# Batch 1's low-rank product of a gated block-sparse layer: sixteen folds replaced by four pairs of seven block products

## The chip, the cores and the metric

The kernel runs on one core of one Trainium2 chip. Its engines are named as in the profile: PE (matrix engine), DVE (vector), ACT (scalar), POOL (GpSimd) and SP (SyncE, which only issues DMAs here). The metric is device time in microseconds (us) of the whole program, as the median of several runs.

## The reference, cut to what matters

`xn` is the layer-normed input `x`, of 2 batches of 1024 rows and 1024 columns. A masked linear layer gives `s`, a linear layer with eight low-rank experts gives the gate `g`, and the output is `x + s * silu(g)`:

```python
xn = _layernorm(x)
s  = einsum('bsk,nk->bsn', xn, weight * blockmask) + bias
q  = einsum('bi,ki->bk', xn.mean(axis=1), Wq)
coeffs = softmax(einsum('bk,ek->be', q, lora_keys) / sqrt(128))     # 8 experts
h     = einsum('bsi,eir->bser', xn, lora_down)                      # rank 64 each
delta = einsum('be,bser,ero->bso', coeffs, h, lora_up)
out   = x + s * silu(einsum('bsi,oi->bso', xn, W_org) + delta)
```

Since the coefficients depend on the batch only, the kernel folds the experts into the weight. With D the 1024 x 512 matrix of all `lora_down`, U the 512 x 1024 matrix of all `lora_up` and C the diagonal of the coefficients (64 equal ones for each expert), batch b is multiplied by the effective weight `W_org^T + D C_b U`, of 1024 x 1024. The term `D C_1 U`, batch 1's low-rank product, is what the change is about.

## The kernel before, in words

All matrix products are made to fp32 accuracy in three passes. An operand is split into a rounded part "hi" (a copy by ACT) and a remainder "lo" (a subtraction by DVE), and a product is hi*hi + hi*lo + lo*hi: three matmuls with a 128x128 stationary and a 128x512 moving operand. "k tiles" are the eight blocks of 128 rows of the weight, "h" its two halves of 512 columns.

The program first prepares batch 0 and multiplies it as plain tiles (`gemm`: 8 k tiles x 3 matmuls for a 128x512 result). Phase y00 and phase y01 are the gate's two halves for batch 0; S tiles 0 to 7 (`s_tile`) are the last half of `s` for batch 0. Batch 1 comes last, as eight units of weight rows, each done by a `quad`: seven block products in place of eight (Strassen's scheme in Winograd's form), with operand blocks `xw[0]` to `xw[3]` (batch 1's input, each of seven block combinations) and `ow` (the weight's). The combinations of the input were stored in DRAM (`xv`) before; `fill(j, m)` loads one, and splits it into `xw[j]`.

Batch 1's effective weight is built between phase y01 and the quads, and goes to DRAM (`yu`), from where the quads' units of kind "y" load it. That is done in 16 *folds*, one for each h and k tile, which stand between the S tiles 0 to 4 in groups of 4, 4, 3, 3 and 2. A fold loads a D tile (`ds`) and a W_org tile (`wo`), splits D into `dhi` and `dlo` (L410, L411), multiplies it with the four scaled U tiles (`y_mul`: 4 chunks x 3 matmuls, L419 to L421), adds the W_org tile on DVE (`y_sum`, L426) and leaves the result to be stored by an ACT-issued DMA (`store_late`, L515) at the next fold. D is loaded and split twice, once for each h. U is scaled by the coefficients while it is split (`scale_up`, L397 and L398): the first half after batch 1's softmax (`coeffs(1)`, of which `steps` are the parts), the second after fold 7.

Between the folds stand fills of `xw[0]` and then `xw[1]`, through three slots of `misc`, and, as `early`, the masking and the block differences of the quads' unit 0. S tiles 5, 6 and 7 come behind the last fold, with unit 0's splits and two fills.

Order: inside the scheduled region PE, DVE, ACT and POOL execute in the order in which the program is written; SP's DMAs are placed by a planner, which may pull a load ahead of its place in the text. An evacuation of a PSUM tile is put into `pending` and written out at the next `flush`. A final evacuation (`final_evac`) is DVE's sum and product, a POOL-issued DMA that adds x into the tile (L507), and an output store, which is issued by ACT at the start of the next S tile but one (`store_out`, L522). On any engine an instruction that waits holds up all that is behind it, DMA issues included.

Buffers that matter: `raw` (seven slots of 128x512), `misc` (three), `stash` (eight, batch 0's gate tiles until their final evacuation), the pool `cu` (five pairs, U's operands), the pool `stage` (D, W_org and weight tiles); PSUM pools `ps_s` and `ps_w` of two banks each and `ps_acc` of four for the S tiles.

Of the kernel before, what the change touches and what calls it, by code (L numbers as in the profile page):

```python
# [9 lines left out]
F32 = mybir.dt.float32  # L10
F32R = mybir.dt.float32r
# [6 lines left out]
P = 128  # L18
# [14 lines left out]
def kernel(  # L33
# [15 lines left out]
):  # L49

# [602 lines left out]
    with tc.manual_schedule(engines={mybir.EngineType.PE, mybir.EngineType.DVE, mybir.EngineType.Activation, mybir.EngineType.Pool}):  # L653
# [350 lines left out]
        def jobs_c(i):  # L1004
# [6 lines left out]
            if i < 6:  # L1011
                yield J(s_mul, s1, 1, i)
            if i == 6:
                yield steps[3]
                yield J(scale_up, 1, 0, up_homes)
# [12 lines left out]
        up_homes = [misc[:, 0, :]]  # L1028
# [4 lines left out]
        folds = [(h, kt) for h in range(2) for kt in range(NKT)]  # L1033

        def fold(n):
            h, kt = folds[n]
            if n + 1 < len(folds):
                y_prep(1, *folds[n + 1])
            store_late()
            y_mul(1, h, kt)  # L1040
            flush()
            y_sum(1, h, kt)
            ps, ws = staged.pop((1, h, kt))
            late_stores.append((
                yu[:, :, 2 * h + kt // 4, kt % 4, :].rearrange("u p n -> p u n"),
                ws.rearrange("p (u n) -> p u n", n=P),
            ))
            if n == NKT - 1:
                homes = [misc[:, (len(spare) + k) % 3, :] for k in range(3)]
                spare.extend(homes)  # L1050
                scale_up(1, 1, homes)

        xw = {}
        XV = (0, 2, 3, 4, 5, 1, 6)

        def fill(j, m, pool=None, at=None):

            if j not in xw:
                home, tag = ((wpool, "w"), (xpool, "xg"), (xpool, "xg"), (wpool, "w"))[j]
                xw[j] = home.tile([P, 7, 2, NH], F32R, name="xw", tag=tag)  # L1060
            if at is not None:
                st = at
            elif pool is None:
                st = misc[:, len(spare) % 3, :]
# [67 lines left out]
        y_prep(1, *folds[0])  # L1132
        done = 0
        filled = [0, 0]

        def fills(j, n):
            for _ in range(n):
                fill(j, ORDER_X[filled[j]])
                filled[j] += 1

        for i, n in enumerate((4, 4, 3, 3, 2)):
            s_tile(i)
            for k in range(n):
                fold(done)
                done += 1
                if i < 3 and k in ((1, 2, 3), (0, 1), (1, 2))[i]:
                    fills(0, 1)
                if i > 2 and (i == 4 or k):
                    fills(1, 1)
                if (i, k) in ((2, 0), (3, 0), (3, 1), (3, 2), (4, 0), (4, 1)):  # L1150
                    early.pop(0)()
            if i == 0:
# [222 lines left out]
```

## Time and profile before

| what | value |
|---|---|
| median of 3 runs | 445.38 us (444.71 to 446.79) |
| the profiled execution | 444.3 us, span in the profile 442.6 us |
| granted PE clock | 1.00 throughout |
| PE busy | 435.9 us, 2053 matmuls |
| DVE, ACT, POOL busy | 288.0, 174.5, 64.9 us |
| DMA | 90.58 MB, mean 205 GB/s |
| S tile 0 to the first quad | 198.25 to 286.3 us of the span |
| folds and S tiles in it | 16 x 12 and 8 x 24 matmuls |

The profile shows one execution, with times from the start of its span. "Busy" counts the time in which an engine has an instruction in work; matmuls overlap, so PE's pace is read from starts of matmuls and not from the duration of one. A row of the groups gives line, engine, operation, output<-input and mean duration. The chain of waits leads back from the last instruction, at each step to whatever released it.

### The profile page before, as it was taken

The numbers are of one execution on the slowest core, as the hardware profiler recorded it, in microseconds if no ns is written. First come the engines' busy times: TensorE is split into PE (matmuls) and PEld (weight loads), VectorE is DVE, ScalarE is ACT, GpSimd is POOL, SyncE is SP. The second block draws the span as 40 slices with busy tenths as digits, with TensorE's granted clock in tenths as the row PEclk, the third lists the DMA queues.
The fourth block names the chain that finished last, engine by engine and source line by source line (L and its number), as shares of the span: only waits on it lengthen the run. The fifth ranks groups of instructions, "written<-read, shape, count | busy, mean of one in ns | idle before, by whom it ended". The sixth has DMA issues, their size and how long they took to land.

```text
span 442.6 us, 5778 instructions
## 1 busy us (share of the span) xinstructions
PE 435.9 (98%) x2053; PEld 362.7 (82%) x2053; DVE 288.0 (65%) x482; ACT 174.5 (39%) x286; POOL 64.9 (15%) x87
## 2 busy tenths in 40 slices
PE   8999999999999999999999999999999999999996
PEld 6899888888888888888888878888888888888885
DVE  5889977765628778974557568378556395365625
ACT  3787435355721221252232135067335322441510
POOL 3342210002310423210000000110020030002000
PEclk9999999999999999999999999999999999999999
DMA  8994616686896899896988986874183146218103
GB/s 282 392 342 158 205 46 228 217 268 218 236 302 177 275 271 319 298 384 166 296 230 262 320 263 185 252 246 142 43 192 118 64 119 168 95 31 214 42 1 118
DMA packets 47741, 90.58 MB, mean 205 GB/s; under 512 B 4816, under 2 KB 15328, under 8 KB 47712
## 3 DMA queue, kind: packets, MB, share of 16 engines
q1 hardware_dynamic: 30624, 66.08, 44.4%
q0 software_dynamic: 6624, 16.26, 15.5%
q10 hardware_dynamic: 10464, 7.87, 5.4%
q8 instruction: 16, 0.26, 0.2%
q14 instruction: 13, 0.11, 0.1%
HBM read 70.26 MB, written 19.93 MB: 204 GB/s over the span
## 4 chain that ended last, share of the span: by engine, by line
PE 91%; DMA 4%; DVE 2%; ACT 1%; issue 1%; POOL 0%; SPq 0%; ACTq 0%; DVEq 0%
PE acc_ps L1220 25%; PE acc_ps L455 13%; PE acc_ps L459 13%; PE acc_ps L458 13%; PE py L1220 10%; PE psw L419 6%; PE psw L421 6%; PE psw L420 6%; DMA ds<-in_down_dram 3%; DMA raw<-in_x_dram 1%; PE pt L209 0%; DVE s L256 0%; ACT slot L592 0%; POOL slot L596 0%; DVE st L148 0%
## 5 line engine op out<-in xcount | busy, mean ns | idle before, releaser
L1220 PE MATMUL acc_ps<-xw,ow 128*128 128x512 f32 (+1 forms) x492 | 111.9, 384 | 0.0
L455 PE MATMUL acc_ps<-slot,xgrp 128*128 128x512 f32 (+1 forms) x288 | 106.5, 370 | 0.1
L1220 PEld LDWEIGHTS acc_ps<-xw,ow 128*128 128x128 f32 x492 | 90.8, 188 | 18.4
L459 PE MATMUL acc_ps<-slot,xgrp 128*128 128x512 f32 (+1 forms) x288 | 105.5, 366 | 0.2 <-DVE xgrp L608 0.2
L458 PE MATMUL acc_ps<-slot,xgrp 128*128 128x512 f32 (+1 forms) x288 | 105.4, 366 | 0.1
L459 PEld LDWEIGHTS acc_ps<-slot,xgrp 128*128 128x128 f32 x288 | 54.3, 188 | 9.6 <-DVE xgrp L608 0.6
L455 PEld LDWEIGHTS acc_ps<-slot,xgrp 128*128 128x128 f32 x288 | 54.3, 188 | 9.4 <-ACT slot L592 0.6
L458 PEld LDWEIGHTS acc_ps<-slot,xgrp 128*128 128x128 f32 x288 | 54.3, 188 | 8.9 <-POOL slot L596 0.3
L419 PE MATMUL psw<-cut,dhi 128*128 128x512 f32 x128 | 49.9, 390 | 0.3 <-ACT dhi L410 0.3
L421 PE MATMUL psw<-cut,dlo 128*128 128x512 f32 x128 | 49.9, 390 | 0.0
L420 PE MATMUL psw<-cut,dhi 128*128 128x512 f32 x128 | 49.8, 389 | 0.0
L1220 PE MATMUL py<-xw,ow 128*128 128x512 f32 x192 | 46.3, 389 | 0.0
L1220 PEld LDWEIGHTS py<-xw,ow 128*128 128x128 f32 x192 | 36.0, 188 | 7.5
L1113 DVE TENSOR_TENSOR ow<-raw,ow 128x1024 fp32r<-128x1024 f32 (+1 forms) x32 | 34.5, 1088 | 8.6 <-ACT ow L1112 8.6
L410 ACT CAST dhi<-ds 128x512 fp32r<-128x512 f32 x32 | 19.7, 616 | 45.6 <-DMA ds<-in_down_dram 30.2
L507 POOL DMA_DIRECT2D stash<-in_x_dram x16 | 14.4, 899 | 119.8 <-DVE stash L504 119.8
L426 DVE TENSOR_TENSOR wo<-wo,psw 128x512 f32<-128x512 f32 x32 | 21.9, 686 | 13.9 <-PE psw L421 13.5
L1112 ACT CAST ow<-raw 128x1024 fp32r<-128x1024 f32 (+1 forms) x32 | 29.4, 939 | 1.6 <-DVE wo L426 1.6
L419 PEld LDWEIGHTS psw<-cut,dhi 128*128 128x128 f32 x128 | 24.0, 188 | 5.7 <-ACT dhi L410 0.7
L411 DVE TENSOR_TENSOR dlo<-ds,dhi 128x512 fp32r<-128x512 f32 x32 | 22.0, 688 | 10.0 <-ACT dhi L410 9.9
L421 PEld LDWEIGHTS psw<-cut,dlo 128*128 128x128 f32 x128 | 24.0, 188 | 5.4 <-DVE dlo L411 0.4
L420 PEld LDWEIGHTS psw<-cut,dhi 128*128 128x128 f32 x128 | 24.0, 188 | 4.9
(182 smaller groups left out, 453.2 us busy)
## 6 DMA issues: line engine op xcount, KB each, us to landing
ds<-in_down_dram SPq DMA_DIRECT2D x32, 256.0 KB, 3.7
wo<-in_worgT_dram SPq DMA_DIRECT2D x32, 256.0 KB, 3.8
raw<-in_x_dram SPq DMA_DIRECT2D x11, 512.0 KB, 4.8
stash<-in_x_dram POOLq DMA_DIRECT2D x16, 256.0 KB, 5.1
raw<-in_wu_dram SPq DMA_DIRECT2D x8, 512.0 KB, 5.1
yu<-wo ACTq DMA_DIRECT2D x16, 256.0 KB, 4.3
raw<-yu SPq DMA_DIRECT2D x8, 512.0 KB, 3.7
out_dram<-stash ACTq DMA_DIRECT2D x14, 256.0 KB, 2.9
```

What stands on the lines that cost most here:

```text
L410: nc.scalar.copy(dhi, ds)
L411: nc.vector.tensor_tensor(dlo, ds, dhi.bitcast(F32), ALU.subtract)
L419: nc.tensor.matmul(ps, lhsT=dhi[:, c, :], rhs=u[c][:, 0, :], start=c == 0, stop=False)
L420: nc.tensor.matmul(ps, lhsT=dhi[:, c, :], rhs=u[c][:, 1, :], start=False, stop=False)
L421: nc.tensor.matmul(ps, lhsT=dlo[:, c, :], rhs=u[c][:, 0, :], start=False, stop=c == 3)
L426: nc.vector.tensor_tensor(ws, ws, ps, ALU.add)
L455: nc.tensor.matmul(ps, lhsT=xs[:, kt, 0, cols], rhs=w[:, kt, 0, wc], start=kt == 0, stop=False)
L458: nc.tensor.matmul(ps, lhsT=xs[:, kt, 0, cols], rhs=w[:, kt, 1, wc], start=False, stop=False)
L459: nc.tensor.matmul(ps, lhsT=xs[:, kt, 1, cols], rhs=w[:, kt, 0, wc], start=False, stop=kt == NKT - 1)
L1112: nc.scalar.copy(o[:, a:b, 0], raw[:, a:b])
L1113: nc.vector.tensor_tensor(o[:, a:b, 1], raw[:, a:b], o[:, a:b, 0].bitcast(F32), ALU.subtract)
L1220: nc.tensor.matmul(ps, lhsT=o[:, a, wl, j, :], rhs=xw[j][:, m, xl, cols], start=start and j == 0 and k == 0, stop=j == 3 and k == 2, skip_ ...
```

## The change

Batch 1's `D C_1 U` is now made in four *pairs*: pair k (`pair`) takes k tiles k and k + 4 and both halves h at once, which is a 2 x 2 block product (rows: k tiles; columns: halves; inner: the 512 ranks in two halves of two chunks). It is made from seven block products of 2 chunks x 3 matmuls, with the same scheme as the quads. The results are added to the four W_org tiles by DVE (`take`), seven sums a pair, and stored by POOL-issued DMAs (`keep`). In PSUM, `px` and `py` are from `ps_s`, `pz` and `pw` from `ps_w`; ACT copies px to pz after the first product.

U is no longer scaled. It is loaded whole into `raw` and `misc` during phase y01 (`up_load`), its block differences are made by DVE (`up_sum`), and its seven combinations for each of two groups are split (`up_split`) during phase y01's last two tiles and S tiles 0 and 1. Their homes are the `cu` pool, the tile "cut2" and `xw[0]`, which is refilled with batch 1's input later. The coefficients are applied to D: ACT scales it chunk by chunk in place (`down_scale`), POOL makes its differences, and `down_split` and `down_rest` split its seven combinations.

The order changes with it: S tiles 0, 1, 2, then pair 0, S tile 3, pair 1, S tile 4, pair 2, S tile 5, pair 3, S tiles 6, 7. W_org's tiles are loaded ahead of their pair: for pairs 0 and 1 into slots of `raw` and `misc`, for pairs 2 and 3 into four `stash` buffers, the same for both. The fills of `xw[1]` stand in pairs 1 to 3, those of `xw[0]` in and behind pair 3, through two slots of `misc` and then the `xs` pool. In the pairs, output stores are issued by POOL. The diff, cut to its core:

```diff
@@ jobs_c (phase y01)
+            if i == 5:
+                yield J(up_load)
             if i == 6:
+                yield from up_jobs[0]
                 yield steps[3]
-                yield J(scale_up, 1, 0, up_homes)
+                yield from up_jobs[1]
+            if i == 7:
+                yield J(down_open)
+                yield J(down_scale, 0)
+                yield from up_jobs[2]
+                yield J(down_split, 0)
...
+        def up_load():
+            for g in range(2):
+                for half, pair in enumerate(((nat7[:, 0:2], nat7[:, 2:4]), (nat7[:, 5:7], misc[:, 0:2]))[g]):
+                    c = g + 2 * half
+                    nc.sync.dma_start(pair.rearrange("p s n -> p (s n)"), up[c * P : (c + 1) * P, :])
...
+        def up_split(g, m):
...
+            nc.scalar.copy(o[:, 0], v)
+            nc.vector.tensor_tensor(o[:, 1], v, o[:, 0].bitcast(F32), ALU.subtract)
...
+        up_jobs = [
+            [S_(0, 3), O_(0, 0), S_(0, 4), O_(0, 1), S_(0, 5)],
+            [S_(0, 6), O_(0, 3), O_(0, 4)],
+            [S_(1, 3), S_(1, 5), O_(0, 5), O_(0, 2)],
+            [O_(0, 6), O_(1, 0), S_(1, 4), O_(1, 3), O_(1, 1), S_(1, 6), O_(1, 4), O_(1, 6), O_(1, 2), O_(1, 5)],
+        ]
...
+        def down_scale(k):
+            d = down_t["raw"]
+            for i in range(2):
+                nc.sync.dma_start(d[:, 2 * i : 2 * i + 2].rearrange("p s c n -> p (s c) n"), down[k + 4 * i])
+            by_chunk = d[:, 0:4].rearrange("p (i s) c n -> p i (s c) n", i=2)
+            for c in range(4):
+                v = by_chunk[:, :, c, :]
+                nc.scalar.activation(v, v, AF.Copy, scale=csel[1][:, c : c + 1])
+            for o, a, b, op in ((4, 2, 3, ALU.add), (5, 4, 0, ALU.subtract), (2, 0, 2, ALU.subtract)):
+                nc.gpsimd.tensor_tensor(d[:, o], d[:, a], d[:, b], op)
...
+        def down_split(k):
+            down_part(0, 2, 0)
+            down_part(4, 6, 4)
+            d = down_t["raw"]
+            nc.gpsimd.tensor_tensor(d[:, 1], d[:, 1], d[:, 5], ALU.subtract)
+        def down_rest(k):
+            down_part(2, 4, 2)
+            down_part(6, 7, 1)
...
+        def worg_load(k):
+            if k < 2:
+                tiles = [nat7[:, 4 * k + j] for j in range(4 - k)] + [misc[:, 2]] * k
+            else:
+                if not worg_late:
+                    worg_late.extend(stash_p.tile([P, NH], F32, name="wo2", tag="stash") for _ in range(4))
+                tiles = worg_late
...
+        def pair(k, jobs):
...
+            mul(0, 0, px, True)
+            nc.scalar.copy(pz, px)
+            then(0)
+            mul(4, 3, py, True)
+            then(1)
+            mul(1, 1, pz, False)
+            take(3, py)
+            then(2)
+            mul(5, 4, px, False)
+            take(0, pz)
+            keep(0)
+            take(1, px)
+            then(3)
+            mul(3, 6, pw, True)
+            then(4)
+            mul(6, 2, py, False)
+            take(2, pw)
+            then(5)
+            mul(2, 5, px, False)
+            take(1, py)
+            keep(1)
+            take(3, px)
+            keep(3)
+            take(2, px)
+            keep(2)
+            then(6)
...
-                st = misc[:, len(spare) % 3, :]
+                st = misc[:, len(spare) % 2, :]
...
+        work = {
+            0: {},
+            1: {4: [F_(1, 1)]},
+            2: {4: [F_(1, 1)], 6: [early[0], early[1]]},
+            3: {1: [F_(1, 1)], 2: [F_(0, 1)], 4: [F_(0, 1)], 6: [F_(0, 1)]},
+        }
+        after = {0: [], 1: [F_(1, 2)], 2: [F_(1, 2)] + early[2:]}
+        for k in range(4):
+            jobs = {n: list(v) for n, v in work[k].items()}
+            if k < 3:
+                jobs.setdefault(0, []).insert(0, J(down_scale, k + 1))
+                jobs.setdefault(3, []).insert(0, J(down_split, k + 1))
+                jobs.setdefault(5, []).append(J(store_out, 0, nc.gpsimd))
+                at = 6 if k == 2 else 5
+                jobs.setdefault(at, []).append(lambda k=k: worg.update({k + 1: worg_load(k + 1)}))
+            jobs.setdefault(1, []).insert(0, flush)
+            pair(k, jobs)
+            if k < 3:
+                s_tile(3 + k)
+                down_rest(k + 1)
+                for job in after[k]:
+                    job()
+                if k == 0:
+                    unit_load(0, 0)
+                    unit_load(0, 1)
...
-        for k in (3, 4, 5, 6):
+        for k in (3, 4):
             for job in for_unit0[k]:
                 job()
-        s_tile(5)
-        for k in range(2):
-            fill(1, ORDER_X[5 + k], xs_pool)
         s_tile(6)
+        fills(0, 1, xs_pool)
+        for k in (5, 6):
+            for job in for_unit0[k]:
+                job()
+        fills(0, 1, xs_pool)
         s_tile(7)
+        fills(0, 2, xs_pool)
```

## Prediction

> **What bounds the kernel now.** I read the engine table first, then the chain of waits, then the stretch that the change touches, then the queues in it. One page line and one chain line say that the matrix engine (PE) is never without work:
>
> ```profile
> PE 435.9 (98%) x2053; PEld 362.7 (82%) x2053; DVE 288.0 (65%) x482; ACT 174.5 (39%) x286; POOL 64.9 (15%) x87
> ...
> PE 91%; DMA 4%; DVE 2%; ACT 1%; issue 1%; POOL 0%; SPq 0%; ACTq 0%; DVEq 0%
> ...
> 310.84 8.16 PE acc_ps L1220 x36
> ```
>
> The last line gives the price of a matmul: 8.16 / 36 = 0.2267 us from start to start (the 389 ns of the groups are latencies that overlap). The touched stretch runs from S tile 0 to the first quad, 198.25 to 286.3 us:
>
> ```profile
> core 0: us, PE busy (x) PEld busy (x) DVE busy (x) ACT busy (x) POOL busy (x), PEclk, DMA share, GB/s
> 198.25:286.30 88.05, 87.74 (x386) 72.04 (x385) 51.57 (x75) 25.08 (x41) 6.20 (x7) 1.00 0.84 251
> ```
>
> It holds 8 S tiles of 24 and 16 folds of 12 matmuls: 384 x 0.2267 = 87.05, so 1.0 us of 88.05 is not matmul work. Its place is in the chain, where a D load came too late for the last but two of the folds:
>
> ```profile
> 241.66 5.97 DMA ds<-in_down_dram
> ...
> 247.73 0.63 ACT dhi L410
> ...
> 248.97 6.05 DMA ds<-in_down_dram
> ...
> 255.13 0.63 ACT dhi L410
> ...
> 255.80 0.50 PE psw L419
> ```
>
> And the waits of the DMA queue in that stretch show why it came late: SyncE (SP) stands still behind loads whose buffer is still being stored.
>
> ```profile
> SPq L407 <- DMA yu<-wo: 21.2, 7, 5.9
> ...
> ACT dhi L410 <- DMA ds<-in_down_dram: 24.6, 9, 6.8
> ```
>
> **PE's part.** Out go 16 folds x 12 = 192 matmuls, in come 4 pairs x 7 products x 6 = 168 of the same shape. 24 x 0.2267 = 5.44 us. The late D load goes too: each D tile is loaded once instead of twice (2 MB fewer of 90.58 MB), and a pair ahead: another 1.0. The S tiles keep their 192 matmuls. Gain 6.44 if all else is hidden. The weight loads (188 ns) stay under the matmuls as now.
>
> **Vector and scalar work.** U was 8 scaled splits (ACT 0.72, DVE 0.75 each); now 14 splits (ACT 0.62, DVE 0.69) and 8 differences (0.69): DVE 15.1 for 6.0, ACT 8.7 for 5.7. The sums into worg rise from 16 to 28 at 0.686 (L426): +8.2 on DVE. D's low parts: 4 x (3 x 0.69 + about 0.42 for 256 elements) = 10.0 for 11.0. Scaling D is new: 16 activations of 256 elements. The trace has no such row; a 256-element cast takes 0.41 and a scaled 512-element activation 0.72, so between 0.41 and 0.72; I take 0.5, 8 us in all, and 4 PSUM copies at 0.57 (L1250). Net: DVE +16, ACT +12, less the 16 issues of 0.37 that leave ACT. DVE's 51.6 of 88 becomes some 62 to 66 of about 82 (part of U's work lies ahead of the stretch): full, not over.
>
> **Before pair 0** the cover is y01's last two tiles and S tiles 0, 1, 2. On DVE from 192.6 (scores done) stand 22 U operations at a 0.62 pitch, the softmax (0.85), D's four low parts (2.3) and two S evacuations (2.8): 19.6, done near 212.2. Pair 0 starts at 198.25 + 3 x 5.44 = 214.6, and its last operand is asked for 8 us later. U's four loads replace eight half-sized ones, two of which landed late only in ACT's queue. Price 0. If the U loads were over 5 us late, this would be the loss, one to one. ACT also stands in S tile 2's output store until S tile 0's accumulate lands (about 209 + 5.1 = 214), and pz's copy is queued behind it, due at 216.0: free by 1 to 1.5 us.
>
> **Inside a pair**, counted from its start: products end every 1.36 us, 9.52 in all, and with the S tile behind it the next pair starts at 14.96. pz's copy runs 1.4 to 2.0 and is due at 2.72: slack 0.8, if nothing blocks ACT. The second use of py is due at 6.80, of px at 8.16; their readers on DVE have 3 to 4 us. So all is hidden except what DVE waits for: the worg tiles. For pairs 0 and 1 they lie in raw and misc, free early. Pair 2's take the stash buffers of S tiles 0 to 3, pair 3's the tiles that pair 2 has just stored. That is the one new wait on the path.
>
> **The wait at pair 3** goes through POOL, in order. Pair 2: ACT scales D until 3.8; POOL makes three 256-element differences (1302 ns at 512 and 2396 at 1024 elements in the groups extrapolate to about 0.76 each), to 6.1; then S tile 4's accumulate is issued (0.88) and lands 5.1 after that (3.7 to 9.0 in L507's answer), 11.2; the output store behind it waits for this landing and blocks POOL; then keep(1) and keep(3) issue at 11.8 and 12.3. A 256 KB store from POOL with 512-byte pieces is not in the trace: from ACT it lands in 4.3, xv stores from POOL in 5.7. So keep(3) lands at 16.6 to 18.0, the load into its tile is issued on SP and takes 3.8: 20.4 to 22.4, pair 3's 5.4 to 7.4. take(3, py) ends 0.7 later and is due at 6.8; behind it on DVE stand a fill's subtraction and two sums (1.9), due at 8.16. Stall 0 to 1.8, and up to 5 if POOL's 0.55 grows with the four-fold pieces; I take 1.6, near the rows. Pair 2's own tile lands at about 4.1 to 6 of that pair against 6.1: 0.
>
> **Going into the quads.** Four fills of the first operand move from the folds to behind S tiles 6 and 7, and only 2 S tiles (10.9 us) are left there where 3 (16.4) stood. They pass through the four xs buffers, which are free only once the last pair has read its weights; so xw[2]'s and xw[3]'s loads, which waited ready before, now follow them with 3.7 to 5 us each. ACT's row says how close this is already:
>
> ```profile
> 287.19 2.18 ACT L1069 CAST xw<-xs 128x512 fp32r<-128x512 f32 x4 [11.47 <-DMA xs<-xv]
> ...
> 290.85 0.57 ACT L1250 COPY acc_ps<-acc_ps 128x512 f32<-128x512 f32 x1
> ```
>
> That copy ended 0.3 us before PE used it at 291.75. Now the third and fourth of these fills land 2 to 4 us after the S tiles' end instead of before it. 0 to 2.5; I take 0.8.
>
> **The sum**: 444.3 (profiled execution; its span is 442.6) - 5.44 - 1.0 + 1.6 + 0.8 = 440.3. The median shown, 445.38, lies 1.08 above that execution: 441.3.
>
> **A rule against it.** The stores of y leave ACT for POOL. The xv stores show what a POOL issue costs beside a DVE that never rests:
>
> ```profile
> 186.37 0.54 POOL L529 DMA_DIRECT2D xv<-bd  x1
> 186.90 1.09 POOL L529 DMA_DIRECT2D xv<-tt  x2
> ...
> 185.89 0.68 DVE L312 TENSOR_TENSOR slot<-ws,slot 128x512 fp32r<-128x512 f32 x1
> ```
>
> The Trainium skill, "SBUF — State Buffer", section "A bandwidth-pool intuition that's wrong (but worth ruling out)", says that a GpSimd-issued DMA of about 620 ns takes about 3100 ns while a DVE copy holds the shared port. By it four POOL issues of the chain above cost about 2.5 more each: pair 3 would wait some 11 us, and the total be about 451. The rows have 0.54 beside two-input subtractions, and this stretch has no DVE copy: I take 0.55. The same page ("Who interferes with whom") makes a GpSimd operation that reads SBUF and a two-SBUF-input DVE operation exclude each other. The trace has no clean overlap of the two; the price would be up to 0.76 per POOL difference, on D's low parts for the next pair, where DVE has slack: 0 taken, inside the range.
>
> **Rivals.** *All hidden*: the store chain and the fills are in time; 445.38 - 6.44 = 438.9. For it: every cover computed above is within 2 us. Against it: accumulates landed up to 9.0 late. *More is late*: POOL issues near 2 us, or both waits at their upper ends, 4 to 8 us: 443 to 447. *Slower: SP's head-of-line blocking reaches pz's copy.* In the S tiles ahead of pairs 2 and 3 two fills stand on ACT in front of that copy. If their loads are queued on SP behind a worg load that waits for a store, they land at 5.5 into pair 2 and 7 into pair 3; two casts (1.24) and the copy (0.57) bring pz to 7.4 and 8.9 where 2.72 is due: 4.7 + 6.2 lost, with the 0.8 above 450.6. For it: the L407 line above, and misc<-xv loads held until 237.82 behind a D load. Against it: those fill loads had gone out up to 20 us ahead of their folds where their buffer was free. It decides once the sum of such delays passes 6.4 us. *It saves no products* (168 not reached) can be excluded from the code: seven calls of six.
>
> **Chances.** Half a per cent, 2.2 us, is about what a measurement of this kernel can tell from no change; so faster is under 443.15, slower above 447.6. All hidden 0.27; the forecast 0.38 (its own range 440 to 443); more is late 0.20; slower 0.15. Faster: 0.27 + 0.37 = 0.64; same 0.20; slower 0.16. The range runs from 438.3 (a full gain with a little luck) to 447.0, leaving out mainly the slower rival.
>
> **What to look for.** PE's count falls by 24 to 2029. Right: no PE wait before pairs 0 to 2, one of 1 to 2 us in pair 3 at py's second use, released by DVE and behind it a worg load. Wrong: PE waiting on ACT at pz's second product (the slower rival); POOL issues of y near 2 us or more; D loads still in the chain; waits on U at pair 0; DVE above 85% in a pair. A quad 0 that waits for xw fills by over 2.5 us breaks the 0.8.

## The result: slower by 4.2%, and the profile after

The changed kernel takes 464.12 us (median of 6 runs, 462.28 to 465.38), beside 445.06 for the kernel before on the same chip: ratio 1.042, 95% interval 1.039 to 1.045. The forecast was 441.3, in a range that ended at 447.0; the sign was wrong. The profiled execution took 465.4 us with a span of 463.7. (Each ratio here leaves disturbed executions out, so it can differ a little from the ratio of the medians beside it. Line numbers shift by a few from kernel to kernel: the pairs' matmuls are L1145 or L1146, `take` is L1151 or L1152, `keep` L1155 or L1156, a fill on ACT L1206, L1207 or L1209.)

The page shows the products gone and the engine waiting:

```profile
PE 438.0 (94%) x2029; PEld 361.7 (78%) x2029; DVE 305.2 (66%) x508; ACT 184.7 (40%) x312; POOL 93.2 (20%) x123
...
PEclk8999999999999999999999995979999999999999
...
PE 59%; issue 16%; DMA 10%; DVE 6%; POOL 5%; ACT 2%; SPq 0%; ACTq 0%; POOLq 0%; DVEq 0%
```

2029 matmuls are the 24 fewer that the sum asked for. But the chain that was 91% PE is 59% PE, and in the row of the granted clock two slices behind the middle are down to 5 and 7 tenths, where the kernel before has a 9 in all 40. (PE's 438.0 us of busy time is no sign of more work: it counts the slow matmuls in full.)

The touched stretch by stage (columns: the stage and its length, busy us and instructions of PE, PE's weight loads, DVE, ACT and POOL, then granted clock, DMA share, GB/s), here pair 0, pair 1, pair 2, pair 3 and the head of quad 0:

```profile
217.00:228.80 11.80, 9.92 (x43) 7.82 (x43) 9.09 (x14) 4.45 (x9) 6.08 (x9) 1.00 0.77 199
...
234.30:243.80 9.50, 9.50 (x43) 7.85 (x42) 4.05 (x6) 2.83 (x6) 2.63 (x4) 1.00 0.62 207
...
249.30:261.10 11.80, 10.12 (x44) 7.73 (x43) 5.82 (x10) 3.44 (x7) 2.86 (x5) 1.00 0.73 237
...
266.80:287.70 20.90, 12.61 (x42) 9.61 (x43) 14.66 (x23) 4.02 (x7) 4.56 (x6) 0.77 0.68 215
...
298.90:316.00 17.10, 10.96 (x40) 8.31 (x39) 8.05 (x13) 7.67 (x14) 1.68 (x3) 0.80 0.78 235
```

A pair is 42 matmuls, 9.52 us. Pair 1 takes exactly that; the others do not, and pair 3 takes 20.9. In the order of time, PE's waits in these stages, each with what released it:

```profile
221.82 0.97 PE L1145 MATMUL psw<-cut,dw 128*128 128x512 f32 x3 [1.88 <-ACT psw L1168]
...
253.52 0.96 PE L1145 MATMUL psw<-cut,dw 128*128 128x512 f32 x3 [1.37 <-ACT psw L1168]
...
282.46 1.65 PE L1145 MATMUL psv<-cut,dw 128*128 128x512 f32 x3 [7.52 <-DVE wo L1151]
283.91 1.48 PE L1145 MATMUL psv<-xw,dw 128*128 128x512 f32 x3
285.19 1.48 PE L1145 MATMUL psv<-cut,dw 128*128 128x512 f32 x3
286.47 1.48 PE L1145 MATMUL psv<-xw,dw 128*128 128x512 f32 x3
...
308.62 1.95 PE L1384 MATMUL acc_ps<-xw,ow 128*128 128x512 f32 x3 [6.14 <-ACT xw L1209]
```

Two waits are for pz's copy on ACT (pairs 0 and 2), one for `take(3, py)` on DVE (pair 3), one for a fill (quad 0). The three rows behind the 7.52 show a second loss: they start 1.28 us apart, 0.427 a matmul, where a warm matmul takes 0.2267.

**The account.** The first quad begins 81.9 us behind pair 0 (217.05 to 298.93), where 4 pairs and 5 S tiles are 4 x 9.52 + 5 x 5.44 = 65.3: 16.6 lost, 2.6 of it in pair 3's last twelve matmuls at the slow pace (5.29 us for 2.72). Quad 0 loses 6.3 and, at the slow pace, 2.0 more. And the execution had come 2.5 us later to batch 1's softmax (`xrow` starts at 188.67, before at 186.15), ahead of the new work; in the runs below that start scatters from 185.6 to 188.6. Together 27.4; less 6.4 for what was saved, 21.0; the spans differ by 21.1.

What stands behind the waits is in POOL's timeline, from pair 2 on:

```profile
264.37 1.14 POOL L1155 DMA_DIRECT2D yu<-wo  x1
265.17 1.11 POOL L1109 TENSOR_TENSOR dr<-dr 128x256 f32<-128x256 f32 x1
267.78 0.58 POOL L523 DMA_DIRECT2D out_dram<-stash  x1 [1.50 <-DMA stash<-in_x_dram]
269.20 0.75 POOL L1155 DMA_DIRECT2D yu<-wo  x1 [0.84 <-DVE raw L1238]
273.08 0.76 POOL L1155 DMA_DIRECT2D yu<-wo  x1 [3.13 <-DVE raw L1246]
276.56 0.75 POOL L1155 DMA_DIRECT2D yu<-wo  x1 [2.72 <-DVE stash L505]
```

The last three y stores are issued in 0.75 us each (the first in 1.14), but they leave 3.5 to 4.8 us apart, though DVE had made the sums that they store by 268.0. (In the first of these gaps POOL also issued an output store, which waited for an accumulate to land; in the other two it issued nothing.) The releasers named in brackets are work of DVE that the stores do not read (masks and block differences of the quads' unit 0, an S tile's evacuation): the profile only names what ended last. And SP, whose W_org loads go into the tiles being stored, waits for those stores (us in total, times, longest):

```profile
SPq L1132 <- DMA yu<-wo: 13.0, 4, 3.6
...
SPq L1132 <- DMA out_dram<-stash: 10.8, 3, 4.5
```

In pair 3 three of the four W_org loads take SP 7.8 us, the fills' loads go out behind them, and on DVE one of these fills stands ahead of the sum that PE waits for:

```profile
268.88 7.76 SPq L1132 DMA_DIRECT2D wo<-in_worgT_dram  x3
276.74 0.85 SPq L1208 DMA_DIRECT2D misc<-xv  x2
...
281.12 0.69 DVE L1210 TENSOR_TENSOR xw<-misc,xw 128x512 fp32r<-128x512 f32 x1 [4.61 <-ACT xw L1209]
281.73 0.68 DVE L1151 TENSOR_TENSOR wo<-wo,psv 128x512 f32<-128x512 f32 x1
```

### The profile page after: what moved, and what is told of

Same layout as the page of the kernel before. It is cut to its first block, busy times and chain, and to the rows that moved or that the text cites. A ratio compares the mean times of both kernels' runs of the same rounds, so it can differ in the third digit from the quotient of the medians.

```text
span 463.7 us, 5788 instructions
## 1 busy us (share of the span) xinstructions
PE 438.0 (94%) x2029; PEld 361.7 (78%) x2029; DVE 305.2 (66%) x508; ACT 184.7 (40%) x312; POOL 93.2 (20%) x123
## 4 chain that ended last, share of the span: by engine, by line
PE 59%; issue 16%; DMA 10%; DVE 6%; POOL 5%; ACT 2%; SPq 0%; ACTq 0%; POOLq 0%; DVEq 0%
PE acc_ps L1384 23%; PE py L1384 9%; PE acc_ps L460 6%; PE acc_ps L459 6%; PE acc_ps L456 6%; DMA stash<-in_x_dram 3%; DMA ws<-in_wT_dram 3%; PE psw L421 2%; PE psw L422 2%; PE psw L420 2%; POOL yu L1155 1%; POOL dr L1095 1%; DMA xs<-xv 1%; PE warm L676 1%; DMA misc<-xv 1%
## 5 line engine op out<-in xcount | busy, mean ns | idle before, releaser
L1384 PE MATMUL acc_ps<-xw,ow 128*128 128x512 f32 (+1 forms) x492 | 113.2, 386 | 6.1 <-ACT xw L1209 6.1
L1367 POOL DMA_DIRECT2D gate<-in_xT_dram x12 | 10.4, 904 | 96.2 <-DVE gate L1361 67.9
L1145 PE MATMUL psv<-cut,dw 128*128 128x512 f32 x60 | 18.6, 421 | 8.2 <-DVE wo L1151 8.2
L1428 DVE TENSOR_TENSOR py<-py,s 128x512 f32<-128x512 f32 x8 | 5.6, 699 | 30.6 <-ACT s L1391 30.6
L420 PE MATMUL psw<-cut,dhi 128*128 128x512 f32 x64 | 24.9, 389 | 0.0
L421 PE MATMUL psw<-cut,dhi 128*128 128x512 f32 x64 | 24.9, 389 | 0.0
L422 PE MATMUL psw<-cut,dlo 128*128 128x512 f32 x64 | 24.9, 389 | 0.0
L430 ACT CAST slot<-wo 128x512 fp32r<-128x512 f32 x16 | 9.9, 621 | 37.5 <-DVE wo L427 33.3
L1246 DVE TENSOR_TENSOR raw<-raw 128x512 f32<-128x512 f32 x32 | 21.3, 688 | 0.6
L1145 PEld LDWEIGHTS psv<-cut,dw 128*128 128x128 f32 x60 | 11.8, 201 | 11.8 <-DVE wo L1151 8.7
```

The lines of the kernel that those rows point to most:

```text
L420: nc.tensor.matmul(ps, lhsT=dhi[:, c, :], rhs=u[c][:, 0, :], start=c == 0, stop=False)
L421: nc.tensor.matmul(ps, lhsT=dhi[:, c, :], rhs=u[c][:, 1, :], start=False, stop=False)
L422: nc.tensor.matmul(ps, lhsT=dlo[:, c, :], rhs=u[c][:, 0, :], start=False, stop=c == 3)
L1145: nc.tensor.matmul(ps, lhsT=w[:, a, wl, c, :], rhs=u[:, ul, :], start=start and c == 0 and n == 0, stop=c == 1 and n == 2, skip_group_chec ...
L1246: nc.vector.tensor_tensor(raw[:, o], raw[:, a], raw[:, b], op)
L1384: nc.tensor.matmul(ps, lhsT=o[:, a, wl, j, :], rhs=xw[j][:, m, xl, cols], start=start and j == 0 and k == 0, stop=j == 3 and k == 2, skip_ ...
```

## Experiments

Times are medians in us, "profiled span" is one execution's, and the waits are PE's longest at each place in that execution. In a quad, "pb's copy" is what pz's copy is in a pair: ACT copies a block product from PSUM to PSUM, and PE adds the next products to the copy.

| run | median (n) | ratio to before, 95% | profiled span | PE waits: pair 0 / 2 / 3 / quad 0 |
|---|---|---|---|---|
| changed kernel | 464.1 (6) | 1.042 (1.039 to 1.045) | 463.7 | 1.9 / 1.4 / 7.5 / 6.1 |
| ring2048 | 455.3 (4) | 1.022 (1.018 to 1.026) | 455.6 | 3.6 / 0 / 2.7 / 2.6 |
| keep_act | 456.1 (4) | 1.026 (1.023 to 1.029) | 453.2 | 0.9 / 0.6 / 3.6 / 2.3 |
| pieces2k | 454.9 (4) | 1.023 (1.018 to 1.028) | 450.5 | 0.5 / 0 / 4.8 / 2.9 |
| pieces_a | 453.2 (4) | 1.021 (1.016 to 1.025) | 449.8 | 0 / 0 / 4.9 / 2.5 |
| pieces_b | 455.3 (4) | 1.025 (1.021 to 1.028) | 453.7 | 1.4 / 0.3 / 4.8 / 3.6 |
| pieces_c | 454.2 (4) | 1.023 (1.021 to 1.026) | 450.9 | 2.2 / 0 / 2.4 / 4.0 |
| pieces_d | 453.3 (4) | 1.020 (1.017 to 1.024) | 452.8 | 1.1 / 0 / 2.8 / 2.9 |
| worg_order | 457.2 (4) | 1.023 (1.015 to 1.031) | 455.5 | 0.6 / 0.7 / 2.9 / 4.2 |
| all_waits | 450.2 (15) | 1.009 (1.006 to 1.013) | 446.6 | 0 / 0 / 2.8 / 3.5 |
| split_late | 449.1 (4) | 1.010 (1.006 to 1.015) | 447.7 | 0 / 3.1 / 0.6 / 1.0 |
| split_late_3slots | 449.7 (4) | 1.012 (1.009 to 1.014) | 446.8 | 0 / 3.0 / 0 / 1.4 |
| split_late_p2 | 445.5 (22) | 1.002 (1.000 to 1.005) | 445.0 | 0 / 0 / 2.4 / 1.5 |
| store_behind | 446.8 (14) | 1.003 (1.000 to 1.006) | 447.3 | 0.5 / 1.1 / 2.6 / 0.4 |
| sums_behind | 447.6 (22) | 1.005 (1.003 to 1.008) | 444.6 | 0 / 0 / 0 / 4.5 |
| copy_first | 447.1 (14) | 1.001 (0.998 to 1.004) | 448.3 | 0 / 1.2 / 0 / 2.2 |

A version's executions scatter by up to 8 us, so differences of 1 or 2 between medians of four runs decide nothing. The waits are of one execution each: what they wait for tells more than their size.

### Do the y stores block POOL? Three ways of taking that away

The theory: POOL writes the descriptors of its DMAs into a space that the program sets to 1024 bytes a partition. A y store, 256 KB in 512 pieces of 512 bytes, fills so much of it that the next store has to wait until the former has gone out. The rivals were that DVE, full DMA engines or the order of the program make them late.

**ring2048**: the space doubled (three small tiles rearranged to make room for it), the order of every engine unchanged.

```diff
...
-SCRATCH = 1024
+SCRATCH = 2048
```

> The changed kernel with twice the space for POOL's DMA descriptors (2048 bytes a partition instead of 1024; two small tiles moved to make room); the order of every engine is the same. Theory (descriptor space): a y store has 512 pieces of 512 bytes, so only one fits at a time, and POOL stands still until the one before has landed: 4 stores a pair x 4 to 5 us. With twice the space three fit: stores of one pair issue under 1 us apart when their data are there, pair 3's wait for worg falls from 7.7 us to 0 to 2, the wait in quad 0 from 6.3 to 0 to 2.5; the time falls to 441 to 448. Rival (DVE holds POOL off the shared port, or the DMA engines are full): the spacing stays at 3 to 5 us and the time at 462 to 465.

**keep_act**: the same stores, issued by ACT.

```diff
             def keep(j):
-                nc.gpsimd.dma_start(
+                nc.scalar.dma_start(
```

> The changed kernel with the y stores issued by ACT, as before the change, at the same places. Both theories of POOL's stores: POOL is free, so output stores, accumulates and D differences come in time, 441 to 448. If instead worg loads and fills are late for SP's own order or for want of DMA bandwidth: waits at pair 3 and quad 0 stay above 4 us each, 455 or more. New price: ACT stands still for a DVE sum ahead of the next D split, which is due only a pair later: 0, but ACT's last store of a pair also stands ahead of the next pair's copy of px.

**pieces2k**: `yu` laid out so that a y store writes 2 KB rows, 128 pieces; the quads' loads of `yu` read 512-byte pieces in exchange.

```diff
-        yu = dram.tile([4, P, 4, 4, P], F32, name="yu")
+        yu = dram.tile([4, 4, P, NH], F32, name="yu")
...
-                nc.gpsimd.dma_start(
-                    yu[:, :, 2 * h + kt // 4, kt % 4, :].rearrange("u p n -> p u n"),
-                    wo[j].rearrange("p (u n) -> p u n", n=P),
-                )
+                nc.gpsimd.dma_start(yu[2 * h + kt // 4, kt % 4], wo[j])
```

> The changed kernel with yu laid out so that a y store writes 2 KB pieces (128 of them instead of 512); the quads' y loads read 512-byte pieces instead (SP). POOL issues them, with the descriptor space as in the changed kernel. Descriptor space: a store takes a quarter of the space, so they issue under 1 us apart: 441 to 448. Shared port or a slow generator for each DMA whatever its pieces: unchanged, 462 to 465. A third case: the price follows the number of pieces written and not the space (issue of one falls below 0.76 and the spacing with it to a quarter, near 1.2 us): same time as the first, but then the run with more space must stay slow.

All three gain 8 to 9 us, and the gaps between the stores are gone. None comes to the 441 to 448 that the theory expected: waits of 2.3 to 4.8 us stay in pair 3 and quad 0. POOL in ring2048, at the end of pair 1 and of pair 2:

```profile
247.65 0.76 POOL L1155 DMA_DIRECT2D yu<-raw  x1
248.40 0.76 POOL L1155 DMA_DIRECT2D yu<-misc  x1
249.15 0.76 POOL L1155 DMA_DIRECT2D yu<-raw  x1
...
265.00 2.24 POOL L1155 DMA_DIRECT2D yu<-wo  x3
```

and in pieces2k, at the same places:

```profile
242.86 0.55 POOL L1155 DMA_DIRECT2D yu<-raw  x1
243.45 0.54 POOL L1155 DMA_DIRECT2D yu<-misc  x1
244.05 0.54 POOL L1155 DMA_DIRECT2D yu<-raw  x1
...
259.65 1.73 POOL L1155 DMA_DIRECT2D yu<-wo  x3
```

The stores follow at 0.75 us with twice the space and at 0.6 with a quarter of the pieces. As ring2048 changes neither their order nor their data, space it was; DVE, the DMA engines and the order are out as the cause of the gaps. The Trainium skill, "DMA: Bandwidth & Descriptors", section "SWDGE vs HWDGE vs iDMA", has these descriptors written by GpSimd into rings in SBUF, which fits; that a full ring holds POOL up, and at which size, only the runs show. How many descriptors a store takes is not in the profile.

That explains 9 of the 19 us. Ten remain, and the waits are at three of the same places.

### The three places that remain, one at a time

Each on pieces2k. **pieces_a**: ACT does not issue S tile 0's output store at the start of S tile 2. **pieces_b**: in pair 2 POOL's output store goes behind the y stores. **pieces_c**: the last four fills of `xw[0]` go through `misc`, not through the `xs` buffers. **pieces_d**: pair 3's fills come later, so that `take(3, py)` has none ahead of it.

```diff
# pieces_a, in s_tile
-            store_out()
+            if i != 2:
+                store_out()
# pieces_b
-                jobs.setdefault(5, []).append(J(store_out, 0, nc.gpsimd))
+                jobs.setdefault(6 if k == 2 else 5, []).append(J(store_out, 0, nc.gpsimd))
# pieces_c
-        fills(0, 1, xs_pool)
+        fills(0, 1)
...
-        fills(0, 2, xs_pool)
...
             if k == 4:
                 flush()
+                fills(0, 2)
# pieces_d
-            3: {1: [F_(1, 1)], 2: [F_(0, 1)], 4: [F_(0, 1)], 6: [F_(0, 1)]},
+            3: {3: [F_(1, 1)], 4: [F_(0, 1)], 5: [F_(0, 1)], 6: [F_(0, 1)]},
```

> The version with 2 KB pieces (454.9 us), and S tile 2 no longer issues S tile 0's output store on ACT: it goes out with a later one on POOL. Theory (ACT stands in that store when pz's copy is due, so PE waits at pz's second product in pair 0): the wait there (0.67 us in the pieces run, 1.88 in the changed kernel) is gone, and the total falls by 0.5 to 3 us, to 452 to 454.5. Rival (POOL, in pair 0, then blocks on two stores and passes the delay on to pair 1): pair 0 or 1 still waits, no gain or a loss.

> The version with 2 KB pieces, and in pair 2 POOL's output store, which waits for an accumulate to land, goes behind the y stores instead of ahead of two of them. Theory (pair 3's wait is set by the chain: pair 2's y stores land, then the W_org loads into the same tiles, then fills behind them on SP): those stores leave about 3 us earlier, pair 3's wait of 4.8 us falls to 1.5 to 3, total 452 to 453. Rival (the fills' own loads set the wait, whatever the stores do): wait unchanged, 454 to 456.

> The version with 2 KB pieces, and the last four fills of the first input operand pass through the misc slots instead of the four xs buffers that the next operands are loaded through, two of them before S tile 6. Theory (quad 0's wait of 2.9 us, and the slower matmuls behind it, come from the xs buffers' being freed late): quad 0 no longer waits, total down by 3 to 5, 450 to 452. Rival (the loads are late because SP is, not because of the buffers): the wait stays or moves to another fill, 454 to 456.

> The version with 2 KB pieces, and pair 3's fills written later, so that on DVE the first sum into a W_org tile is ahead of all of them. Theory (the sum stands on DVE behind a fill whose load SP issued behind the four W_org loads): the wait in pair 3 falls from 4.8 us to that of the W_org load itself, 1 to 3 us, total 451 to 453.5. Rival (the W_org load is the last to come anyway): wait unchanged. Risk on the other side: fills of the first operand come later and quad 0 waits longer.

pieces_a did what was expected: no wait in pair 0. In the changed kernel ACT shows the cause (ACTq is its issue of a DMA):

```profile
220.81 0.34 ACTq L523 DMA_DIRECT2D out_dram<-stash  x1
221.19 0.57 ACT L1168 COPY psw<-psv 128x512 f32<-128x512 f32 x1 [3.19 <-DMA stash<-in_x_dram]
```

The copy was ready earlier and stood behind the store, which stood 3.2 us for an accumulate to land. Without that edit this wait is 0.5 to 3.6 us over the runs, so it also adds to the scatter of the medians.

pieces_b was a miss: pair 3's wait stayed at 4.8. pieces_d had 2.8 there: in pieces2k the sum that PE waited for stood on DVE behind a fill, whose load stood on SP behind the four W_org loads, and in pieces_d it follows DVE's former work at once. But the size does not prove it. The sum starts at 270.8 in both traces, and PE only came to pair 3 1.95 us later (261.74, 259.79). pieces_c, which changes nothing up to there, came 4.4 later and waited 2.4. pieces_c moved quad 0's wait from a fill to pb's copy (4.0 us), which now stood on ACT behind the last `misc` fill: a miss.

### What is left of pair 3: the W_org load, or DVE?

**worg_order**: pieces_a and pieces_d, and pair 3 takes pair 2's buffers in the order in which they are stored.

```diff
-                tiles = worg_late
-            for j, t in enumerate(tiles):
+                tiles = worg_late if k == 2 else [worg_late[n] for n in (1, 3, 2, 0)]
+            for j in (3, 0, 1, 2) if k == 3 else range(4):
+                t = tiles[j]
```

> The version with 2 KB pieces, S tile 2 without its output store on ACT, pair 3's fills written later, and one thing new: pair 3 takes pair 2's W_org buffers in the order in which pair 2 stores them (its first sum, tile 3, uses the buffer of pair 2's tile 0, the last, tile 2, that of the last stored), and loads them in that order. Theory (what is left of pair 3's wait, 2.8 us, is the load of the tile that is summed first, behind the store of the tile that was stored last but one): the first of the four loads leaves some 3 us earlier, pair 3 waits 0 to 0.5 and has no slow matmuls behind the wait, total 448 to 450. Quad 0 keeps its 3 us and the slow matmuls. Rival (pair 3 is bound by the fills on DVE and ACT, or DVE itself is late from pair 2): the wait stays at 2.5 to 3, total 452 to 454.

**all_waits**: the same and the `misc` fills of pieces_c, with the third slot of `misc` in use from pair 3 on.

```diff
-                st = misc[:, len(spare) % 2, :]
+                st = misc[:, len(spare) % slots[0], :]
...
+            if k == 3:
+                slots[0] = 3
             pair(k, jobs)
```

> The one before, and the last four fills of the first input operand pass through misc, through three slots from pair 3 on. Theory (all of the 10 us that the version with 2 KB pieces is over the kernel before, and the 6 that the products save, were these three places, pair 0, pair 3 and quad 0): no wait on PE of over 1 us is left, and the total is 438 to 442, faster than before. Rival (each place that is mended shows the next transfer, since the DMA queue of SP has no room left: the fills of two operands, W_org and the unit's loads in a shorter stretch): a wait of 2 us or more stays at quad 0, total 444 to 448.

worg_order fell to its rival, with the wait in pair 3 as long as in pieces_d and the median no lower. all_waits gained (450.2), and kept a wait of 2.8 in pair 3 and of 3.5 in quad 0. DVE's timeline of all_waits tells why the earlier load did not help. In pair 2:

```profile
254.79 0.74 DVE L1100 TENSOR_TENSOR dw<-dr,dw 128x512 fp32r<-128x512 f32 x1 [2.08 <-ACT dw L1099]
256.82 0.69 DVE L1100 TENSOR_TENSOR dw<-dr,dw 128x512 fp32r<-128x512 f32 x1 [1.28 <-ACT dw L1099]
257.43 2.12 DVE L1208 TENSOR_TENSOR xw<-misc,xw 128x512 fp32r<-128x512 f32 x1
259.47 0.68 DVE L1152 TENSOR_TENSOR wo<-wo,psw 128x512 f32<-128x512 f32 x1
260.07 1.87 DVE L1152 TENSOR_TENSOR wo<-wo,psv 128x512 f32<-128x512 f32 x3
...
270.32 0.68 DVE L1152 TENSOR_TENSOR wo<-wo,psv 128x512 f32<-128x512 f32 x1
```

DVE stands 3.4 us in D's splits, waiting for what POOL and ACT make of a D tile that came late; the pair's last four sums are queued behind and end at 261.9, 6 us after the last product. From there DVE works without a pause until 270.3, when it starts the sum that PE waits for. DVE is the releaser because it is late.

**split_late**: all_waits, with D's split at the end of each pair. **split_late_3slots**: three `misc` slots from pair 2 on as well.

```diff
-                jobs.setdefault(3, []).insert(0, J(down_split, k + 1))
+                jobs.setdefault(6, []).insert(0, J(down_split, k + 1))
# split_late_3slots also
-                st = misc[:, len(spare) % slots[0], :]
+                st = misc[:, (0, 1, 0)[len(spare)] if len(spare) < 3 else (2, 1, 0)[len(spare) % 3], :]
```

> The version before (all_waits, 450.2 us, profiled span 446.6), with one move: the split of D for the next pair goes from behind the fourth product to the end of each pair, so that DVE takes up the sums of the pair first. Theory (what is left of pair 3's wait, 2.8 us, is DVE being late from pair 2, where it stood 3.4 us idle in D's splits, waiting for the differences on POOL, with four sums queued behind; those sums late make the y stores late, these the W_org loads, and these all that SP has behind them): DVE reaches pair 3's first sum some 3 us earlier, the wait in pair 3 is under 0.5, the W_org loads leave SP 3 us earlier, and quad 0's wait falls from 3.5 to 1 or 2; total 443 to 447. Rival (the W_org load in pair 3 or its fills' loads are the last to come): pair 3 waits 2 us or more as before, total 449 to 452; or D's split is now late for the next pair's first product, and PE waits there on DVE or ACT.

> The one before, with the fills going through three slots of misc from pair 2 on and not only from pair 3. Theory: two fills more can be loaded ahead of pair 3's W_org loads on SP, so the fills in pair 3 no longer stand behind them; 0 to 2 us less than split_late, 442 to 446. Rival (the third slot is free only when pair 1's last W_org tile is stored, and the fill's load now waits for that on SP, with D's loads behind it): no gain, or up to 2 us more.

Pair 3's wait for the sum went from 2.8 to 0.6 and 0: DVE's lateness it was. The medians, 449.1 and 449.7, stay above what was expected. But pair 2 now waits 3 us for pz's copy, since pair 1's move puts POOL's last D difference behind the y stores. The third slot changed nothing in the median. **split_late_p2** makes the move in pair 2 alone:

```diff
-                jobs.setdefault(6, []).insert(0, J(down_split, k + 1))
+                jobs.setdefault(6 if k == 2 else 3, []).insert(0, J(down_split, k + 1))
```

> The version all_waits (450.2 us), with D's split moved to the end of the pair in pair 2 alone; pairs 0 and 1 have it behind the fourth product again. Theory (the late split freed pair 3, and the 3.1 us that PE then waited in pair 2 came from the same move in pair 1, where D's split goes behind the y stores on POOL): both waits are under 1 us, quad 0 keeps 1 to 2 us; the profiled span is 440 to 442.5 and the median 441 to 445, so no more than the kernel before and possibly 2 us less. Rival (DVE, POOL and SP are full in this stretch, so that the lateness only moves on): a wait of 2 us or more stands in pair 3 or quad 0, total 447 to 450.

445.5: level with the kernel before (ratio 1.002), not faster. In its trace the move has its price in pair 3: D's last difference stands on POOL behind the y stores (263.22), and PE waits 2.4 us for pz's copy.

### Is the saving there at all?

**store_behind**: split_late_p2 with the edit of pieces_b. **sums_behind**: the same, and the four block differences of unit 0 go from ahead of pair 3 to behind its last sum. **copy_first**: the same, and the seventh of the fills ahead of quad 0's first copy goes behind it.

```diff
# sums_behind
-            3: {3: [F_(1, 1)], 4: [F_(0, 1)], 5: [F_(0, 1)], 6: [F_(0, 1)]},
+            3: {3: [F_(1, 1)], 4: [F_(0, 1)], 5: [F_(0, 1)], 6: [F_(0, 1)] + early[2:]},
-        after = {0: [], 1: [F_(1, 2)], 2: [F_(1, 2)] + early[2:]}
+        after = {0: [], 1: [F_(1, 2)], 2: [F_(1, 2)]}
# copy_first
-        for k in range(7):
+        for k in range(6):
...
+        last = J(fill, *todo.pop(0), xs_pool, raw[:, 6].rearrange("p j n -> p (j n)"))
...
+        behind[0].insert(0, last)
```

> The version split_late_p2 (445.5 us, profiled span 445.0), and in pair 2 POOL's output store, which stands 2.6 us waiting for an accumulate to land, goes behind the y stores and behind D's last difference. This move alone did nothing on the version with 2 KB pieces (pieces_b), where DVE's sums were as late as the store. Theory (now the sums are early, and the store is the one thing that holds the y stores, and through D's last difference and ACT the copy of px in pair 3): y stores of pair 2 leave by 260 instead of 263.2, pair 3 has no wait over 0.5, total down by 3 to 4, to 441 to 443, which is faster than the kernel before. So the products' saving is real and needs every cover. Rival (another wait takes its place, as each time so far): a wait of 2 us or more in pair 3 or quad 0, total 444 to 446.

> The version store_behind (446.8 us, profiled span 447.3), and the four block differences of the quads' unit 0 (2.73 us of DVE, ahead of pair 3's first sum) go behind pair 3's last sum. Theory (what is left in pair 3 is DVE itself, which works without a pause from 259 to 277 us of that span, so that its sum for the waiting product is 2.6 us late): no wait over 0.5 in pair 3 and no slow matmuls behind it, total down by 3 to 4.5, to 442 to 444; it may give 1 back in quad 0. Rival (DVE's work is only pushed into the last two S tiles, where it is full as well): quad 0 waits 2 to 3 us more, total unchanged at 445 to 447.

> The version sums_behind (447.6 us, profiled span 444.6, no wait left in the four pairs), with one fill less ahead of quad 0's first PSUM copy on ACT: the last of the seven, whose load waits for a raw slot and of which PE needs the operand only four products later, goes behind that copy. Theory (ACT's order: the copy was ready and stood 1.8 us behind this fill's load): quad 0's wait falls from 4.5 us to 2 or 2.5, with little or no slow pace behind it, total down by 2 to 4, to 443.5 to 445.5, level with the kernel before or up to 1.5 us below it. Rival (the two fills before it come as late, since all three raw slots are freed by unit 0's split on DVE): the wait stays at 3.5 or more, total 446 to 448.

None beat the kernel before, but the trace of sums_behind answers the question. In that execution (446.3 us) no pair waits, and from S tile 0 to the first quad PE never rests:

```profile
198.24:280.30 82.06, 82.06 (x362) 67.63 (x361) 64.58 (x93) 33.63 (x63) 30.17 (x43) 1.00 0.74 232
256.00:288.00 32.00, 30.25 (x132) 24.12 (x130) 30.69 (x45) 14.15 (x24) 9.48 (x15) 1.00 0.90 281
280.30:296.00 15.70, 10.89 (x37) 8.13 (x36) 12.04 (x20) 8.53 (x15) 2.97 (x4) 0.78 0.95 279
```

Before, this stretch took 88.05; now 82.06. So the saving is real, 6.0 us of the 6.4 forecast. The second row is the price: DVE is busy 30.7 of 32 us around pair 3 and the last S tiles, and the DMA engines 0.90. The third is where it is paid:

```profile
291.05 10.12 PE L1390 MATMUL acc_ps<-xw,ow 128*128 128x512 f32 x33 [4.52 <-ACT acc_ps L1420]
```

pb's copy (L1420) stands on ACT behind a fill, whose load goes into a slot of `raw` that DVE's split of unit 0 frees (until 281.06). SP issued it at 283 to 284, and the fill had its data at 289.9, with the DMA engines busy at 0.95. So sums_behind did what its theory said in pair 3 and what its rival said in quad 0. copy_first took the copy from behind that fill. In its profiled execution, the slowest of its 14, the wait there was 1.4, and one of 2.2 came for ACT's next copy out of PSUM (L1397). The median hardly moved (447.1 after 447.6): neither expectation holds in full. How much of the loss in quad 0 is the order of the queues, and how much the slow landing of loads on full DMA engines, no run separates. store_behind's wait was its rival's: the y stores left at 261 to 263, and pair 3 waited 2.6 us for DVE, which had no pause from 259 to 277.

## Why the prediction was wrong, step by step

- **PE's part** (5.44 + 1.0): right. 2029 matmuls, and the stretch 6.0 us shorter once nothing in it waits (sums_behind).
- **The wait at pair 3** (1.6): the step that failed. The place and the releaser were right, `take(3, py)` on DVE with a W_org load and a store behind it, and a fill between; the size was 7.5 and 2.6 at the slow pace. Two terms were wrong. First, the working let keep(1) and keep(3) issue at 11.8 and 12.3 after pair 2's start. They left at 19.9 and 23.8 (269.20 and 273.08, pair 2 starting at 249.27), since a y store of 512 pieces does not leave POOL in 0.55 us when another is under way: pair 1's last one held POOL until 261.07, 11.8 after the start, and keep(3) came 3.9 behind keep(1). I took that 0.55 from the xv stores, which have 128 pieces, and allowed for growth only in the issue itself (it became 0.75), not in the wait for space. Second, "ACT scales D until 3.8" assumed a D tile loaded by the pair's start. In the changed kernel ACT was done at 10.6 (259.88): half of D's load stood on SP behind a W_org load, which waited 3.6 us for an output store of POOL. In all_waits, where no store blocks POOL, D's buffer came free only 0.7 us before pair 2's start, when the former D was split (245.55), the load landed at 252.4, and ACT was done at 7.9 (254.1). In the other versions it was 1.4 to 7.5 us late. (A slip beside it: 18.0 + 3.8 is 21.8 and not 22.4, so that the working's own range ends at 1.3 and not 1.8.)
- **The vector work** ("full, not over"; 62 to 66 of about 82): the mean was right, 64.6 of 82.1 in sums_behind. The step missed that a mean hides the order: DVE stands idle in pair 2 behind D's splits, then is full for up to 18 us, just where PE needs its sums. The 85% that was to be the sign of it failed as a sign: PE's own wait lengthens the pair, so that pair 3 shows 14.66 of 20.9 in the changed kernel, and 8.35 of 9.52, 88%, in sums_behind, where no pair waits.
- **Before pair 0** (price 0, slack 1 to 1.5 us): wrong. S tile 0's accumulate was to land at 214 and ACT's store was released by it at 220.8; the wait was 1.9, and up to 3.6 in other runs. The accumulate left POOL at 216.13 and not at 209, since S tile 0's evacuation stood on DVE behind splits of U and D, and these were late: the last of U's ended at 218.9 where the working had 212.2. 2.5 us of that is the execution's late start; part of the rest is that ACT stood 4.2 us until D's load landed (203.7), with splits of U behind it. pieces_a removes the wait.
- **Going into the quads** (0.8): wrong by size. 6.3 us and 2.0 at the slow pace in the changed kernel, and a wait of 4.5 when everything ahead of it is in time (sums_behind). In these traces the four fills, the copies of quad 0, unit 0's splits and SP's loads follow on each other through ACT, DVE and SP; I had counted only the `xs` buffers. What would remove this wait stays open.
- **Slow matmuls after a wait**: not in the sum at all, 2.6 us in pair 3 and 2.0 in quad 0.
- **The slower rival** (fills ahead of pz's copy) did happen, with 1.4 us in pair 2 of its 4.7 and 0.6 in pair 3 of its 6.2; the largest loss, the 7.5 us at `take(3, py)` and the slow pace behind it, was in none of them at that size. "More is late" named POOL, and priced all of it at 4 to 8 us, at most a third of the 24.9 that came (16.6 + 6.3 + 2.0).
- **The rule against it**, 3100 ns for a POOL-issued DMA beside DVE, was rightly left out: no y store took more than 1.14 us to issue. The other rule of that page was priced at 0 too soon. A fill's subtraction takes 0.69 alone and 2.12 beside POOL's issue of a y store and a D difference (all_waits, 257.43), on an engine that then has no slack.

## What to carry to other kernels

Before a store is moved to GpSimd, count its pieces: the price of its issue says nothing about how long the next one waits for descriptor space. Before products are traded for combinations, lay out the in-order queues of all the other engines over the shorter stretch, not their mean load: here 6 us of matmuls were bought with work that left DVE without a pause, and each wait that was mended came back at the next queue. A wait of PE over some 2 us can cost up to 3 us more behind it.

## What the runs showed of the hardware that I had not expected

- **A blocked GpSimd DMA queue looks like idle POOL with an unrelated releaser.** With 1024 bytes a partition, y stores of 512 pieces left 3 to 5 us apart, with 2048 bytes 0.75, and with 128 pieces 0.6.
- **The clock after a wait.** Behind the waits of 7.5 (changed kernel), 4.8 and 2.9 (pieces2k) and 3.1 us (split_late), some 8 to 12 matmuls start about 0.427 us apart where a warm one takes 0.2267, and the granted clock of pair 3 is 0.77. No wait under 2 us did this by itself; of waits between 2.2 and 2.9 some did (pieces_c, pair 0) and some did not (all_waits, pair 3). The Trainium skill, "TensorE: Matmul & The Clock Gate", Part 1, gives half the clock after an idle window of about 3.4 us that runs free of the program, and full clock after as much busy time. The pitch agrees with that, and so does the slow stretch of 3.8 to 5.7 us, between one such window and two. That waits of 2.2 to 2.9 us are sometimes enough, the page does not say; here the traces decide.
- **POOL and DVE on SBUF.** Beside POOL's issue of a y store and a D difference, the fill's two-input subtraction took 2.12 us (all_waits, 257.43) against 0.69, and the difference 1.06 against 0.74. "SBUF — State Buffer", section "Who interferes with whom", of the Trainium skill states that two such instructions contend; how the 1.43 us divide between issue and difference is not shown. In the trace of before no clean overlap was found.
